# Four stacked graph-attention layers: score operands of layer 0 in PSUM, in place of one-instruction weights and woven block ends in layers 1 to 3

## The chip, the cores and the metric

The kernel runs on one core of a Trainium2 chip. The metric is device time in microseconds (us), from the first to the last instruction of one execution. Lower is better. A core has five engines that run side by side and wait for each other by semaphores: TensorE (PE, matrix products into PSUM; PEld is its loading of weights), VectorE (DVE, elementwise and reductions), ScalarE (ACT, one activation function with a scale and a bias), GpSimd (POOL; here it issues gathers and scatters by index) and SyncE (SP, issues plain transfers).

## The reference, cut to what matters

3327 nodes with 256 features; a symmetric 0/1 adjacency matrix with ones on the diagonal, with about 1% of its entries set. Each of four layers computes `x = layernorm(x + gnn(x, adj))`; the layers differ in how a pair's score is made.

```python
# layer 0: the score is not separable, a sum over 256 channels for each pair
g_src = x @ W_src.T + b_src;  g_tgt = x @ W_tgt.T + b_tgt
score = einsum('ijc,c->ij', leaky_relu(g_src[:, None] + g_tgt[None], 0.2), a_w)
gnn   = softmax(where(adj, score, -inf)) @ g_tgt

# layer 1: one head, e_ij = leaky_relu(s1_i + s2_j, 0.2)
Wh = x @ W.T;  s1 = Wh @ a1;  s2 = Wh @ a2
gnn = softmax(where(adj, e, NEG)) @ Wh

# layer 2: the same without the leaky_relu
# layer 3: two layers of 4 heads of 64 columns (called 3a and 3b here), each head as in layer 1
h   = einsum('nf,hfd->hnd', x, W)
e   = leaky_relu(f1[:, :, None] + f2[:, None, :], 0.2)
out = elu(einsum('hnm,hmd->hnd', softmax(where(adj, e, NEG)), h))   # 3b reads 3a's out
```

## The kernel before

Rows are handled in 26 tiles of 128 nodes.

**Layer 0** uses the sparse structure. For every tile it makes lists of neighbours (VectorE, from the adjacency matrix), sorts the rows of a group of tiles by the length of their lists, and gathers the neighbours' rows from DRAM by index. There are three groups, of 5, 8 and 13 tiles; `LEVELS` gives how many neighbours are gathered for each tile of a group after sorting (923 gathers of 128 rows in all). A tile's gathers are cut into parts of up to 8; there are 126 parts. `leaky_relu(s + t)` is written as `max(t, -s)` and terms that are linear.

```python
SETS = (5, 8, 13)
LEVELS = {5: (56, 38, 34, 32, 28), 8: (56, 40, ...), 13: (56, 41, ...)}
GROUP, TURNS, LEAD = 8, 11, 4

def gather(q):                       # GpSimd: one part
    if k0 == 0:
        own = io0.tile([P, OWN], F32, tag="own", name="own_of", bufs=4)
        nc.gpsimd.indirect_dma_start(out=own, in_=own_d[s], ...)
    g = gath.tile([P, GROUP, ROW], F32, tag=f"g{q % TURNS}", name="g")
    for k in range(k0, k1):
        nc.gpsimd.indirect_dma_start(out=g[:, k - k0, :], in_=table_d, ...)
        if k % 2 and between:
            between.pop(0)()         # a list written out, or a result put back

def largest(y, rows, minus_src, m):  # VectorE, four neighbours at once
    nc.vector.tensor_tensor(
        y, rows, minus_src[:, None, :].to_broadcast([P, m, dim]), op=ALU.max)

def weighted(y, sc):                 # VectorE, one neighbour: a score of each row
    nc.vector.scalar_tensor_tensor(
        y, y, 1.0, a_row, op0=ALU.mult, op1=ALU.mult, accum_out=sc)

# score(q): largest(..., own[:, :dim], m), then weighted(y, sc[...]) for each of the part
# combine(s, t): softmax weights, ScalarE scales each gathered row, TensorE adds them up
# add_input(s, t): divide, add the input; put_back(s, t): GpSimd scatters the rows
```

VectorE also makes the lists of the groups to come, spread over the parts that precede them. A group's lists are written out by GpSimd (`write_list`), once VectorE has ranked all its rows (`ranks_i`):

```python
for s in range(1, len(SETS)):
    at = begins[s] - LEAD - 1
    at_step(at, read_lists, s)
    at -= SETS[s] // 4 + 1
    for it in range(SETS[s]):
        at_step(at, between.append, lambda s=s, it=it: write_list(s, it))
    ahead.append(neighbours(s))
    owed[at] = steps                 # its lists are due by part `at`
```

**Layers 1 to 3** are dense. The output rows are cut into four blocks of 7, 7, 6 and 6 tiles. For a block, and for each of the 26 tiles `j` of source nodes (a step), a weight tile `e` is made and multiplied on TensorE. The exponential of a leaky_relu is split into factors of row and column, so that a weight is a maximum times the adjacency:

```python
def weigh(self, j, b, at, h_of):
    q = self.feat[j][:pn, ...]
    e = edges.tile([P, wide], F32, tag="e", name="e", bufs=8)
    nc.vector.scalar_tensor_tensor(
        e[:pn, : c1 - c0], self.rate[b][:pn, h_of, : c1 - c0], q,
        at[:pn, : c1 - c0], op0=ALU.max, op1=ALU.mult)
    return e
```

In layer 3, a block's end is short: ScalarE copies the accumulators out, and everything after is a generator in `pending`, advanced by one piece (`work_off`) in each step of the next block:

```python
def many_heads(layer, nxt, finish):
    for b, block in enumerate(blocks):
        work_until(lambda: layer.rate[b] is not None)
        accs = [[bank(3 * x + y) for y in range(pairs + 1)] for x in range(len(parts))]
        for j in range(nt):
            at = adjacent(j, b)
            es = [layer.weigh(j, b, at, h_of) for h_of in range(layer.nh)]
            # ... per part and head: products into accs[x][p] (L1184)
            # ... per part and head: sums of the weights into accs[x][pairs] (L1192)
            if j == 0 or j >= LATER:
                work_off()
        work_until(lambda: not pending)
        o = turn_p.tile([P, pairs, wide], F32, tag="ht", name="o")
        # ... nc.scalar.copy(o..., accs...), nc.scalar.copy(sums..., accs...)
        pending.append(finish(b, o, sums))
```

`finish_hidden` (3a) turns the sums so that rows lie on partitions (L1227), takes reciprocals of 28 or 24 columns (L1233), spreads them back by TensorE (L1266), multiplies, applies elu, and projects each tile for 3b (L998, then its rates, L1035), in stages of two tiles. `finish_last` (3b) turns the rows back (L1312), scales, applies elu, adds the residual, and normalises. The layer norms of layers 1 and 2 (`norms`) are such generators too, at the head of `prepare`, which turns (L1091) and projects (L998) each tile of a block for the next layer. In layer 3 the order of VectorE and ScalarE is the program's own; before it, that of TensorE alone is.

Of the kernel before, what the change touches and what calls it, by code (L numbers as in the profile page):

```python
# [32 lines left out]
SETS = (5, 8, 13)  # L33
LEVELS = {
    5: (56, 38, 34, 32, 28),
    8: (56, 40, 37, 35, 33, 31, 29, 27),
    13: (56, 41, 38, 37, 35, 34, 33, 32, 31, 30, 28, 27, 25),
# [9 lines left out]
def gat_stack(  # L47
# [84 lines left out]
    def dots(work, dst, weight, row, nh):  # L132

        for c in range(kc):
            t = work.tile([P, dim], F32, tag="spread", name="dots", bufs=4)
            nc.vector.tensor_mul(t, weight[:, c, :dim], row)
            nc.vector.tensor_reduce(
                dst[:, c, :], t.rearrange("p (h d) -> p h d", h=nh), axis=AX.X, op=ALU.add
            )
# [68 lines left out]
    def norms(block, ys):  # L208
# [4 lines left out]
        for s, it in enumerate(block):  # L213
# [4 lines left out]
            if s == len(block) // 2:  # L218
                yield
        yield from scaled(block, ys, mv)  # L220

    def scaled(block, ys, mv):
# [5 lines left out]
        yield  # L228
        for s, it in enumerate(block):
# [5 lines left out]
            if s == len(block) // 2:  # L235
                yield
        yield
# [12 lines left out]
    def sparse0(lost):  # L250
        GROUP, TURNS, LEAD = 8, 11, 4
        starts = [sum(SETS[:s]) for s in range(len(SETS))]
        with ExitStack() as s0:
# [3 lines left out]
            ps0 = s0.enter_context(tc.tile_pool(name="s_ps", bufs=2, space=PSUM))  # L257
            s0.enter_context(
# [89 lines left out]
            def sources(it):  # L348

                xt, pn = columns_of(it)  # L350
                pss = ps0.tile([P, BANK], F32, tag="ps", name="pss")
# [23 lines left out]
            def neighbours(s):  # L375
# [8 lines left out]
                for t in range(size):  # L384
# [7 lines left out]
                    for b, (lo, hi) in enumerate(halves):  # L392
# [23 lines left out]
                        for c in range(chunks):  # L416
                            if c == chunks // 2:
                                next(before if b else of_rows, None)
# [116 lines left out]

            def largest(y, rows, minus_src, m):
# [4 lines left out]
            def weighted(y, sc):  # L541

                nc.vector.scalar_tensor_tensor(  # L543
                    y, y, 1.0, a_row, op0=ALU.mult, op1=ALU.mult, accum_out=sc
# [9 lines left out]
            def score(q):  # L554
# [3 lines left out]
                own, g, kt = entry["own"], entry["g"][k0 // GROUP], places[s, t]  # L558
                y_own = None
                if k0 == 0:  # L560
# [9 lines left out]
                    largest(y_own, own[:, None, 2 * dim : 3 * dim], own[:, :dim], 1)  # L570
# [7 lines left out]
                for lo in range(k0, k1, 4):  # L578
# [3 lines left out]
                        y[:, :m, :], g[:, lo - k0 : lo - k0 + m, :dim], own[:, :dim], m  # L582
# [3 lines left out]
                if k0 == 0:  # L586
                    weighted(y_own[:, 0, :], sc[:, kt : kt + 1])
# [6 lines left out]
                for i, y in enumerate(ys):  # L594
                    weighted(y, sc[:, k0 + i : k0 + i + 1])
# [134 lines left out]

            for q, key in ends.items():
# [228 lines left out]
    def layers(rs):  # L960
# [15 lines left out]

        class Layer:
# [14 lines left out]
            def project(self, j, ht, banks):  # L992
# [10 lines left out]
                if self.leaky:  # L1003
                    f = feats.tile([P, dim + 2 * heads], F32, tag=f"{self.slot}{j}", name="feat")
                    nc.scalar.activation(f[:pn, dim : dim + nh], last, AF.Exp)
                    nc.scalar.activation(
                        f[:pn, dim + nh : dim + 2 * nh], last, AF.Exp, scale=SLOPE - 1.0
                    )
                    for lo in range(0, dim, width):
                        nc.scalar.activation(  # L1010
# [478 lines left out]
```

## Time and profile before

Three runs: 3377.6, 3378.3 and 3379.95 us; median 3378.3. The profiled execution spans 3378.2 us.

| engine | busy us | share |
|---|---|---|
| TensorE, products | 2265.2 | 67% |
| VectorE | 2332.9 | 69% |
| ScalarE | 722.5 | 21% |
| GpSimd | 1142.6 | 34% |

| stretch, us | stage |
|---|---|
| 0 to 180 | layer 0: table of target rows, lists of group 0 |
| 180 to 1618 | layer 0: gathers, scores, sums |
| 1618 to 1750 | layer 1 is prepared and begins |
| 1750 to 2304 | layers 1 and 2 |
| 2304 to 2841 | layer 3a |
| 2841 to 3378 | layer 3b, with a tail of 24 us after the last block |

The costliest groups (busy us; mean ns of one): gathers on GpSimd 1012.1 (1097); weights of layer 3 on VectorE 844.9 (1080); products of layer 3 on TensorE 663.5, its sums 333.5; weightings of layer 0 on VectorE 329.2 (419), maxima 278.5 (1180).

How to read it: the shares are averages over stages with different limits, so each part of the change has to be read in its own stretch. GpSimd works in layer 0 only; TensorE sets the pace only after it. The profile puts idle time down to what ended it: "issue" is idle time with nothing to wait for. A busy TensorE can hide a wait, as the ends of its products are modelled: a group of 16 that takes 4.68 us where others take 3.23 has waited inside.

### The profile page before, as it was taken

Reading aid. Unit: us, or ns where it says so; the run is one execution under the profiler, and the core shown is the slowest. Engines: PE = TensorE matmul, PEld = TensorE weight load, DVE = VectorE, ACT = ScalarE, POOL = GpSimd, SP = SyncE. Lnnn points to the kernel's source line nnn. Section 1 sums busy time; section 2 is a strip of 40 time slices with the busy share of each in tenths; the row PEclk is TensorE's granted clock in tenths of the full one; section 3 lists DMA queues with packets and bytes.
Section 4 is the critical chain, followed back from the end, with each engine's and each line's share of the span. In section 5 each row is a group of like instructions: output and inputs, shape, how many; then the busy total and the mean of one; then the engine's idle time right before and its main releaser. Section 6 shows DMA issues by size and latency. Waiting matters only on the chain.

```text
span 3378.2 us, 37935 instructions
## 1 busy us (share of the span) xinstructions
PE 2265.2 (67%) x12318; PEld 1185.5 (35%) x12318; DVE 2332.9 (69%) x6589; ACT 722.5 (21%) x1950; POOL 1142.6 (34%) x1034
## 2 busy tenths in 40 slices
PE   3203342533323443333799999999999999999997
PEld 2101111211111111111378888784333343333332
DVE  6789999999945555555235552117778788789997
ACT  0002221413212332333243431110110110110110
POOL 0177778777677777776000000000000000000000
PEclk6556675766666666766699999999999999999998
DMA  7465545444335333343367663332212212211111
GB/s 214 130 137 175 152 144 147 147 142 136 84 101 117 98 104 105 103 109 94 90 194 212 194 174 94 100 98 70 61 44 63 60 43 62 61 45 56 54 45 46
DMA packets 176816, 363.79 MB, mean 108 GB/s; under 512 B 33746, under 2 KB 118948, under 8 KB 176610
## 3 DMA queue, kind: packets, MB, share of 16 engines
q1 hardware_dynamic: 96682, 183.56, 19.2%
q0 software_dynamic: 49632, 141.57, 16.2%
q10 hardware_dynamic: 30296, 36.15, 3.1%
q8 instruction: 100, 1.64, 0.2%
q14 instruction: 106, 0.87, 0.1%
HBM read 320.99 MB, written 43.58 MB: 108 GB/s over the span
## 4 chain that ended last, share of the span: by engine, by line
PE 46%; DVE 4%; DMA 2%; ACT 1%; issue 1%; POOL 0%; DVEq 0%; ACTq 0%; POOLq 0%; SPq 0%
PE acc L1184 17%; PE acc L1146 14%; PE acc L1192 9%; PE misc L998 3%; DVE e L1062 2%; PE misc L1035 1%; DMA at_i<-in_adj_t_dram 1%; PE misc L1091 1%; DMA at<-at_d 1%; ACT feat L1010 0%; PE acc L626 0%; PE misc L1266 0%; PE misc L1227 0%; DVE stats L1341 0%; DVE h L1339 0%
## 5 line engine op out<-in xcount | busy, mean ns | idle before, releaser
L526 POOL DMA_INDIRECT g<-table_d,lst x923 | 1012.1, 1097 | 289.1 <-issue 269.7
L1062 DVE SCALAR_TENSOR_TENSOR e<-rate,feat,at 128x896 f32<-128x896 f32 (+4 forms) x832 | 844.9, 1080 | 100.9 <-PE acc L1192 91.8
L626 PE MATMUL acc<-g,ident 128*128 128x512 f32 (+1 forms) x936 | 455.1, 644 | 667.0 <-ACT g L623 611.1
L1184 PE MATMUL acc<-e,feat 128*64 128x384 f32 (+4 forms) x3328 | 663.5, 520 | 3.2 <-DVE e L1062 1.7
L225 POOL TENSOR_TENSOR rstds<-rstds,minus_half 128x7 f32<-128x7 f32 (+1 forms) x12 | 19.6, 1632 | 1711.0 <-DVE rstds L224 1711.0
L626 PEld LDWEIGHTS acc<-g,ident 128*128 128x128 f32 x936 | 194.2, 212 | 909.0 <-ACT g L623 671.8
L537 DVE TENSOR_TENSOR y<-g,own_of 128x1024 f32<-128x1024 f32 (+2 forms) x240 | 278.5, 1180 | 311.7 <-DMA g<-table_d,lst 293.2
L1184 PEld LDWEIGHTS acc<-e,feat 128*64 128x64 f32 (+1 forms) x3328 | 236.2, 136 | 391.7 <-issue 269.2
L623 ACT ACTIVATE g<-g,w 128x256 f32<-128x256 f32 x923 | 370.6, 493 | 0.0
L1192 PE MATMUL acc<-e,feat 128*32 128x384 f32 (+4 forms) x3328 | 333.5, 518 | 0.0
L543 DVE SCALAR_TENSOR_TENSOR y<-y,a_row 128x256 f32<-128x256 f32 x923 | 329.2, 419 | 0.0
L1146 PE MATMUL acc<-feat,e 128*128 128x257 f32 (+2 forms) x1352 | 308.3, 382 | 0.6 <-DVE h L1160 0.6
L1146 PEld LDWEIGHTS acc<-feat,e 128*128 128x128 f32 (+2 forms) x1352 | 253.8, 190 | 39.8 <-issue 4.1
L465 PE MATMUL key_rows<-key_diag,ones 128*128 128x128 f32 x52 | 18.3, 450 | 342.0 <-DVE key_diag L464 287.1
L1146 PE MATMUL acc<-feat,at 128*128 128x257 bf16 (+2 forms) x2028 | 241.1, 276 | 7.5 <-DMA at<-at_d 7.2
L612 ACT ACTIVATE w<-sc,top 128x57 f32<-128x57 f32 (+14 forms) x26 | 8.5, 326 | 1093.8 <-DVE top L609 1093.8
L1146 PEld LDWEIGHTS <-at 128*128 128x128 bf16 (+2 forms) x2028 | 200.3, 100 | 43.9 <-DMA at<-at_d 8.0
L1062 DVE SCALAR_TENSOR_TENSOR e<-rate,feat,at_i 128x896 f32<-128x896 f32 (+2 forms) x104 | 112.3, 1082 | 145.8 <-DMA at_i<-in_adj_t_dram 112.2
L420 DVE MAX8 cand<-num 128x8 f32<-128x64 uint16 x1352 | 179.5, 209 | 1.0
L1192 PEld LDWEIGHTS acc<-e,feat 128*32 128x32 f32 (+1 forms) x3328 | 86.6, 108 | 226.6 <-issue 226.6
L465 PEld LDWEIGHTS key_rows<-key_diag,ones 128*128 128x128 f32 x52 | 12.2, 284 | 356.9 <-DVE key_diag L464 266.9
L1079 ACT CAST at<-at_i 128x896 bf16<-128x896 int32 (+2 forms) x104 | 92.0, 885 | 112.6 <-DMA at_i<-in_adj_t_dram 111.0
(156 smaller groups left out, 1709.8 us busy)
## 6 DMA issues: line engine op xcount, KB each, us to landing
at<-at_d SPq DMA_DIRECT2D x150, 224.0 KB
at_i<-in_adj_t_dram SPq DMA_DIRECT2D x50, 448.0 KB
adj_i<-in_adj_dram SPq DMA_DIRECT2D x25, 832.0 KB
adj_i<-in_adj_dram SPq DMA_DIRECT2D x25, 831.5 KB
g<-table_d,lst POOLq DMA_INDIRECT x923, 2.9
at<-at_d SPq DMA_DIRECT2D x75, 192.0 KB
at<-at_d SPq DMA_DIRECT2D x75, 191.8 KB
at_d<-at ACTq DMA_DIRECT2D x50, 224.0 KB
```

Of the source, the lines that this page charges most:

```text
L420: nc.vector.max(cand[:, lo // CHUNK + c, :], v[:, c * CHUNK : (c + 1) * CHUNK])
L526: nc.gpsimd.indirect_dma_start(out=g[:, k - k0, :], out_offset=None, in_=table_d[:, :], in_offset=bass.IndirectOffsetOnAxis(ap=entry["lst" ...
L537: nc.vector.tensor_tensor(y, rows, minus_src[:, None, :].to_broadcast([P, m, dim]), op=ALU.max)
L543: nc.vector.scalar_tensor_tensor(y, y, 1.0, a_row, op0=ALU.mult, op1=ALU.mult, accum_out=sc)
L623: nc.scalar.activation(rows, rows, AF.Copy, scale=w[:, k : k + 1])
L626: nc.tensor.matmul(dst, ident, rows, start=start, stop=stop)
L998: nc.tensor.matmul(pacc[:pn, : dim + nh], ht[:, k, :pn], self.weight[:, k, :], start=(k == 0), stop=(k == kc - 1),)
L1062: nc.vector.scalar_tensor_tensor(e[:pn, : c1 - c0], self.rate[b][:pn, h_of, : c1 - c0], q, at[:pn, : c1 - c0], op0=ALU.max, op1=ALU.mult,)
L1079: nc.scalar.copy(at[:pn, :w], at_i[:pn, :w])
L1146: nc.tensor.matmul(accs[s][:pn, : dim + 1], a[:pj, s * P : s * P + pn], f[:pj, : dim + 1], start=(j == 0 and part == 0), stop=(j == nt - 1 ...
L1184: nc.tensor.matmul(accs[x][p][q * hd : (q + 1) * hd, : hi - lo], f[:pj, h_of * hd : (h_of + 1) * hd], es[h_of][:pj, lo:hi], start=(j == 0) ...
L1192: nc.tensor.matmul(accs[x][pairs][h_of * 32 : (h_of + 1) * 32, : hi - lo], f[:pj, dim + h_of : dim + h_of + 1].to_broadcast([pj, 32]), es[ ...
```

## The change

In **layer 0** the operands that all scores of a tile share, the negated source rows and the row `a_w`, are copied into a PSUM bank by ScalarE, so that the maxima and the weightings on VectorE read only one operand from SBUF. [...] The banks for it are taken from the sorting of the groups: a group may have 12 tiles at most, so the groups become 5, 9 and 12, and a tag of two banks keeps one.

```diff
-SETS = (5, 8, 13)
+SETS = (5, 9, 12)
...
-                pss = ps0.tile([P, BANK], F32, tag="ps", name="pss")
+                pss = ps0.tile([P, BANK], F32, tag="ps", name="pss", bufs=1)
...
+            def lay_out(q):
+                (s, t), _, _ = parts[q]
+                entry = held[s, t]
+                both = entry["both"] = ps0.tile([P, 2, dim], F32, tag="both", name="both")
+                nc.scalar.copy(both[:, 0, :], entry["own"][:, :dim])
+                nc.scalar.copy(both[:, 1, :], a_row)
...
-            def weighted(y, sc):
+            def weighted(y, sc, a):
...
+                minus_src, a = entry["both"][:, 0, :], entry["both"][:, 1, :]
...
+            for q, (key, k0, _) in enumerate(parts):
+                if k0 == 0:
+                    at_step(max(q - 2, 0), lay_out, q)
```

In **layers 1 and 3** a different scheme is taken out. The maximum is a relu on ScalarE and the product is VectorE's second half: `max(r q, 1) = relu(r q - 1) + 1`, with the factors of row and column exchanged to fit.

```diff
+                nc.scalar.activation(
+                    e[:pn, : c1 - c0], self.rate[b][:pn, h_of, : c1 - c0], AF.Relu,
+                    bias=minus_one[:pn], scale=q,
+                )
                 nc.vector.scalar_tensor_tensor(
-                    e[:pn, : c1 - c0], self.rate[b][:pn, h_of, : c1 - c0], q,
-                    at[:pn, : c1 - c0], op0=ALU.max, op1=ALU.mult,
+                    e[:pn, : c1 - c0], e[:pn, : c1 - c0], 1.0, at[:pn, : c1 - c0],
+                    op0=ALU.add, op1=ALU.mult,
                 )
```

A block's end in layer 3 is no longer woven into the next block. Reciprocals are taken of the accumulated sums as they lie (512 or 384 columns), and product and elu are made straight from the accumulators; the next block starts when nothing is pending. The norms are emitted at once, not in pieces, and VectorE and ScalarE are ordered by the scheduler in layer 3 too.

```diff
-                work_until(lambda: layer.rate[b] is not None)
+                work_until(lambda: layer.rate[b] is not None and not pending)
...
-                    if j == 0 or j >= LATER:
+                    if j >= LATER:
                         work_off()
                 work_until(lambda: not pending)
...
+                    inv = work.tile([P, BANK], F32, tag="invs", name="invs", bufs=1)
+                    nc.vector.reciprocal(inv[:, :w], accs[x][pairs][:, :w])
                     for p in range(pairs):
-                        nc.scalar.copy(o[:, p, lo:hi], accs[x][p][:, : hi - lo])
...
+                        spread = misc((6, 7))
+                        nc.tensor.matmul(
+                            spread[:, :w], select[:, p, :], inv[:, :w], start=True, stop=True
+                        )
+                        s = work.tile([P, BANK], F32, tag="spread", name="spread_s")
+                        nc.scalar.copy(s[:, :w], spread[:, :w])
+                        v = o[:, p, lo:hi]
+                        nc.vector.tensor_tensor(v, accs[x][p][:, :w], s[:, :w], op=ALU.mult)
+                        nc.vector.tensor_scalar_min(s[:, :w], v, 0.0)
+                        nc.scalar.activation(s[:, :w], s[:, :w], AF.Exp)
+                        nc.vector.scalar_tensor_tensor(
+                            v, s[:, :w], -1.0, v, op0=ALU.add, op1=ALU.max
+                        )
+                pending.append(finish(b, o))
...
-        def finish_hidden(b, o, sums):
+        def finish_hidden(b, o):
+            for it in blocks[b]:
+                l3b.project(it, o[:, :, at0 : at0 + P], (6, 7))
                 yield
             l3b.rates_of(b, o, (6, 7))
             yield
...
+        def finish_last(b, o):        # per tile: turn back on TensorE, add; then norms at once
...
-        rs.enter_context(
-            tc.manual_schedule(
-                engines={
-                    mybir.EngineType.PE, mybir.EngineType.DVE, mybir.EngineType.Activation
-                }
-            )
-        )
```

In a projection, the scaling of the features by their exponential is one VectorE instruction in place of one ScalarE instruction for each head (L1010). What is left out here is the text of the stages of `finish_hidden` and `finish_last` that go, and the loss of the `yield`s in `norms`.

## The prediction

> **What bounds the kernel now.** I read first the table of busy time by stretch, because one kernel holds four layers with different limits. Its columns: the stretch in us from the start, its length, busy us (and instructions) of PE, PEld, DVE, ACT and POOL, the granted TensorE clock, DMA share and GB/s.
>
> ```profile
> 300.00:500.00 200.00, 68.09 (x157) 32.89 (x155) 194.88 (x871) 44.27 (x113) 156.04 (x136) 0.65 0.52 152
> 900.00:1100.00 200.00, 72.07 (x153) 32.40 (x151) 107.98 (x401) 56.02 (x143) 155.20 (x149) 0.67 0.43 104
> ...
> 1750.00:1960.00 210.00, 209.41 (x979) 182.51 (x979) 116.99 (x234) 79.64 (x137) 4.27 (x3) 1.00 0.70 204
> 1960.00:2307.00 347.00, 336.30 (x2515) 281.35 (x2514) 78.95 (x224) 67.06 (x224) 5.59 (x4) 0.99 0.40 114
> 2307.00:2844.00 537.00, 534.78 (x3659) 194.41 (x3658) 439.22 (x462) 63.38 (x224) 2.10 (x1) 1.00 0.20 55
> 2844.00:3378.00 534.00, 514.24 (x3544) 183.56 (x3542) 468.71 (x569) 66.29 (x206) 7.63 (x4) 0.98 0.18 51
> ```
>
> Layer 0 (to 1620 us) has two parts. Until 889 us VectorE is 97% busy, as neighbour lists are made beside the scores; after that GpSimd alone is full: 155 us busy, and 0.30 us in front of each of its 149 instructions, which is 200 of 200. From 1750 us TensorE works without a gap.
>
> Next, the timeline of layer 0, GpSimd and VectorE: start, duration, engine, line, operation.
>
> ```profile
> 725.14 0.95 POOL L526 DMA_INDIRECT g<-table_d,lst  x1 [0.30 <-issue]
> 726.40 1.06 POOL L526 DMA_INDIRECT g<-table_d,lst  x1 [0.30 <-issue]
> 726.62 2.34 DVE L537 TENSOR_TENSOR y<-g,own_of 128x1024 f32<-128x1024 f32 x2
> 727.76 2.36 POOL L526 DMA_INDIRECT g<-table_d,lst  x1 [0.30 <-issue]
> ...
> 889.23 1.00 POOL L487 DMA_INDIRECT lists_d<-payload,ranks_i  x1 [9.79 <-DVE inv L648]
> ```
>
> A gather alone takes 0.95 us; the one beside two maxima with both inputs in SBUF takes 2.36. The last line is the hinge of the layer: GpSimd writes out the lists of group 2 only when VectorE has ranked them.
>
> Then a block's end in layer 3, TensorE only:
>
> ```profile
> 2444.98 1.71 PE L1192 MATMUL acc<-e,feat 127*32 127x512 f32 x16
> 2446.62 3.66 PE L1184 MATMUL acc<-e,feat 128*64 128x512 f32 x16
> 2450.21 1.71 PE L1192 MATMUL acc<-e,feat 128*32 128x512 f32 x16
> 2451.85 1.73 PE L1227 MATMUL misc<-heads_at,sums 128*128 128x4 f32 x14
> 2453.51 3.23 PE L1184 MATMUL acc<-e,feat 128*64 128x512 f32 x16
> ```
>
> A step is 3.23 + 1.71 less overlap, 4.80 us from start to start; between two blocks only 0.43 us is lost (3.66 for 3.23). The finish of a block lies piecemeal between the next block's steps.
>
> [...] `row<-pt,bt_row` from PSUM has median 418 ns, the `y_own` maximum from SBUF 416; `minus<-pss` from PSUM 406, the weighting from SBUF 420. [...] when layer 1 is prepared (1640 to 1660 us) the clock is 0.50, and a tile's projection takes 2.08 us where it takes 1.03 at 1.00:
>
> ```profile
> 1640.84 0.69 PE L1091 MATMUL misc<-ident,h 128*128 128x128 f32 x2 [0.77 <-ACT feat L1010]
> 1641.56 0.37 ACT L1094 COPY ht<-misc 128x256 f32<-128x256 f32 x1 [0.78 <-PE misc L1091]
> 1641.99 2.08 PE L998 MATMUL misc<-l1w,ht 128*128 128x257 f32 x4 [0.46 <-ACT ht L1094]
> ...
> 1644.84 0.69 PE L1091 MATMUL misc<-ident,h 128*128 128x128 f32 x2 [0.77 <-ACT feat L1010]
> ```
>
> One tile of such a chain, with one PSUM bank, takes 4.00 us. [...]
>
> ```profile
> L1233 DVE RECIPROCAL invs<-misc x8: 274/312/328, 2467.4 to 3355.7; 128x28 f32<-128x28 f32 x4, 128x24 f32<-128x24 f32 x2, 128x20 f32<-128x20 f32 x2
> ```
>
> 328 ns for 28 columns and 274 for 20 make about 7 ns a column.
>
> **The change in layer 0.** The maxima and the weightings read one operand from PSUM, so they stop holding up gathers. Three terms.
>
> (a) VectorE's full part. Groups of 9 and 12 tiles move the ranking of the last group from part 55 to part 59 (of 126). Four more parts cost 4 x 5.2 us (two maxima 2.28, eight weightings at 0.345, small ones 0.16) and one tile's combining 2.5: +23. Ranks: -1. The 4 us that VectorE waited for gathers go. So 889 becomes 907. [...]
>
> (b) GpSimd's full part. Before, 520 instructions from 889.2 to 1590.8: 1.349 us each. After, 448 gathers in place of 479, 487 instructions in all, at 0.95 + 0.30 and 10 us of waits: 619. So 917 + 619 = 1536 in place of 1591: **-55 us**.
>
> (c) ScalarE's two copies into PSUM a tile (26 x 2 x about 0.4) lie on an engine with 1094 us of idle time in this layer: 0.
>
> **The change in layers 1 to 3.** Weights take a second instruction, on ScalarE. From its 256-column form (0.403 us start to start) and 0.8 ns a column I estimate 0.92 us for 896 columns, 3.7 in a step of 4.80 (0.81, 3.25 in 4.16 for six tiles): it fits. VectorE still has one instruction of 1.07. What costs is the block end: a block now starts only when nothing is pending, normalising accumulators and ELU is done straight out of them, with reciprocals 512 and 384 wide.
>
> Seven-tile block of layer 3a, between its last matmul and the next block's first: VectorE, by the order of the built program, has two reciprocals (3.7 + 2.8), five weights (5.3), four products (2.4), four minima (1.3), four ELU ends (2.3), two feature scalings (1.0): 18.8. Then three projections at half clock (3 x 2.1) and two rate products (3.6 + 2.7, as in layer 1's preparation): 32; and 2.5 for the clock to come back: 34.5. The work that TensorE did before for the same finish between its steps, 15.0 (1.65 + 3.3 + 7.0 + 3.1), falls out: +19.5. Six tiles: 16.5 + 0.4 + 6.3 + 5.4 + 2.5 = 31 less 13.1, +18. Two of each: **+75**.
>
> Layer 3b: the same VectorE chain, then only transposes: 19 + 2 + 2.5 less 4.9 = 18.6, twice, and 21 less 4.2 = 16.8 once; 3 more as norms come ahead of weights: **+57**. Last block: 24 us of tail become 32: **+8**.
>
> Layer 2 to 3a: the last block of layer 2, of six tiles, must be normalised (9.5 us), turned and projected (6 x 4.00), and give its rates (7) before a step is made: 40.5 + 2, less 12.3 that was woven in: **+30**.
>
> What is gained back: from 2303.9 to 3354.2, 1050 us, there are 104 steps of 4.80 and 104 of 4.16 (931) and 82 of finishing work on TensorE; **37** were lost in steps that waited for weights because the finishes share VectorE (3.23 stretched to 4.68 or 5.16). These go. Layer 1: ScalarE has 0.94 + 0.92 + about 1.2 in a step of some 3.3 to 3.6: +5.
>
> Sum: 75 + 57 + 8 + 30 - 37 + 5 = +138; with layer 0, 138 - 55 = +83: 3378 + 83 = **3461 us**.
>
> **The rivals.** *Layer 0 wins.* If all 136 us of stretch (1012 less 923 x 0.95) came back, and TensorE kept its clock at the ends (about 50 less), the sum would be near -50: 3330. Against it: before 889 us VectorE is the limit, so stretch there is free. [...] *The weights' chain binds.* The eight buffers make ScalarE, then VectorE, refill within a step: by my count the fourth weight is there 5.5 us after its buffer is free and is needed after 6.0 (six tiles: 4.9 and 5.2). If it fails by 0.2 us a step, 208 steps add 40: 3500. *The ends are hidden after all.* If VectorE's chain overlaps better or the clock stays up, ends cost 10 each and the sum is near +20: 3400. TensorE's unbroken 534.78 of 537 leaves nothing for them to hide under, so I think it the less likely.
>
> **Range and chances.** The layer 0 term I trust to 25, the layer 3 terms to 35; together 40. So 3461, with 3405 to 3512 eight times in ten. 2% is 3446: slower by more 0.64, within 0.34, faster by more 0.02.
>
> **What would show it.** Right: gathers with mean near 0.95 to 0.98 (1.097 now); the last gather ends near 1536; the weighting still 420 ns; steps of 4.80 and 4.16 inside blocks; a hole of 28 to 35 us on TensorE at each of the ends of layer 3a, 20 to 24 in 3b, with clock 0.5; about 42 between layers 2 and 3. Wrong: [...] holes under 15, reciprocals of under 1 us, or steps over 5.

## The result, and the profile after

The changed kernel takes **3402.2 us** (median of 4 runs, 3399.8 to 3405.0) beside 3377.95 us for the kernel before: a ratio of **1.0072, 95% interval [1.0055, 1.009]**, 24 us slower. Predicted were 3461 us and a range from 3405 to 3512. The direction was right, the size (83 us) was 3.4 times too large.

First the table of busy time by stretch, of the changed kernel, with the columns explained in the prediction. Layer 0 now ends at 1540 us (1617 before) and layer 2 at 2242 (2304 before), so the stretches are cut at its own borders.

```profile
900.00:1100.00 200.00, 74.66 (x152) 33.36 (x152) 121.93 (x447) 63.24 (x162) 147.61 (x155) 0.66 0.46 108
...
2242.00:2282.00 40.00, 22.38 (x46) 9.77 (x48) 16.16 (x40) 4.44 (x20) 2.03 (x1) 0.56 0.07 18
2282.00:2836.00 554.00, 525.52 (x3469) 202.03 (x3466) 457.74 (x489) 437.97 (x494) 0.00 (x0) 0.97 0.19 53
2836.00:3372.00 536.00, 509.81 (x3416) 191.27 (x3419) 459.84 (x544) 422.59 (x448) 4.27 (x3) 0.96 0.18 49
```

In layer 0 GpSimd finishes 155 instructions in 200 us where it had finished 149. A stretch of 40 us between layers 2 and 3 is new, at a mean clock of 0.56. In layer 3 TensorE lost its unbroken row: 525.52 of 554.

The hinge of layer 0, from the timeline of the changed kernel (start, duration, engine, line, operation): a gather beside two maxima, and the first write of group 2's lists.

```profile
724.36 2.34 DVE L537 TENSOR_TENSOR y<-g,both 128x1024 f32<-128x1024 f32 x2
...
726.10 0.97 POOL L518 DMA_INDIRECT g<-table_d,lst  x1 [0.30 <-issue]
...
905.77 1.00 POOL L479 DMA_INDIRECT lists_d<-payload,ranks_i  x1 [10.34 <-DVE inv L649]
```

The gather that starts under the maxima takes 0.97 us where one took 2.36; the mean of all 923 is 0.989 us for 1.097. The lists come at 905.8 where they came at 889.2.

Last a block's end in layer 3a, TensorE alone, which answers to the block end of before:

```profile
2403.01 3.23 PE L1193 MATMUL acc<-e,feat 127*64 127x512 f32 x16
2406.17 1.71 PE L1201 MATMUL acc<-e,feat 127*32 127x512 f32 x16
2410.82 3.64 PE L1217 MATMUL misc<-invs,select 128*128 128x512 f32 x4 [2.94 <-DVE invs L1214]
2419.13 2.90 PE L1217 MATMUL misc<-invs,select 128*128 128x384 f32 x4 [4.67 <-DVE invs L1214]
2421.82 8.19 PE L1005 MATMUL misc<-l3bw,o 128*128 128x260 f32 x28
2429.94 3.17 PE L1043 MATMUL misc<-o,w_src 128*4 128x512 f32 x8
2433.04 3.23 PE L1193 MATMUL acc<-e,feat 128*64 128x512 f32 x16
```

From the end of the last step (2406.17 + 1.71 = 2407.88) to the next block's first product (2433.04) it is 25.2 us; 34.5 were predicted. TensorE waits for both reciprocals, the bracketed 2.94 and 4.67 us. The seven projections then take 8.19 us together, 1.17 each, where one takes 1.03 at full clock; and the products of the new block's first step take 3.23 us at once.

Added up by stage, from the first and last products of each stage in the two traces (spans 3378.2 and 3402.1):

| Stage | before | after | measured | predicted |
|---|---|---|---|---|
| layer 0, to its last accumulation | 1616.9 | 1539.8 | -77 | -55 |
| preparing layer 1 | 58.6 | 61.5 | +3 | 0 |
| layers 1 and 2 | 628.5 | 640.5 | +12 | +5 |
| gap ahead of layer 3 | 0 | 39.9 | +40 | +42.5 |
| layer 3 | 1050.3 | 1091.0 | +41 | +83 |
| tail | 23.9 | 29.4 | +5 | +8 |
| sum | | | +24 | +83 |

The predicted 83 in layer 3 is 75 + 57 for the ends, less 37 for the waits, less the 12.3 of work that leaves its first block, which the prediction had booked with the gap.

### The profile page after: what moved, and what is told of

The parts are those of the page before. It is cut to its first block, busy times and chain, and to the rows that moved or that the text cites. A ratio compares the mean times of both kernels' runs of the same rounds, so it can differ in the third digit from the quotient of the medians.

```text
span 3402.1 us, 38429 instructions
## 1 busy us (share of the span) xinstructions
PE 2284.6 (67%) x12068; PEld 1212.8 (36%) x12068; DVE 2372.5 (70%) x6714; ACT 1560.5 (46%) x2546; POOL 1027.9 (30%) x1034
## 3 DMA queue, kind: packets, MB, share of 16 engines
q1 hardware_dynamic: 96682, 183.56, 18.8%
## 5 line engine op out<-in xcount | busy, mean ns | idle before, releaser
L1068 ACT ACTIVATE e<-rate,minus_one,feat 128x896 f32<-128x896 f32 (+2 forms) x936 | 942.4, 1070 | 185.8 <-PE acc L1201 149.7
L518 POOL DMA_INDIRECT g<-table_d,lst x923 | 913.2, 989 | 297.4 <-issue 266.2
L1072 DVE SCALAR_TENSOR_TENSOR e<-e,at 128x896 f32<-128x896 f32 (+4 forms) x832 | 819.5, 1024 | 169.5 <-ACT e L1068 152.4
L1193 PE MATMUL acc<-e,feat 128*64 128x384 f32 (+4 forms) x3328 | 639.6, 525 | 0.0
L537 DVE TENSOR_TENSOR y<-g,both 128x1024 f32<-128x1024 f32 (+2 forms) x240 | 276.2, 1174 | 238.5 <-DMA g<-table_d,lst 222.6
L1193 PEld LDWEIGHTS acc<-e,feat 128*64 128x64 f32 (+1 forms) x3328 | 262.5, 138 | 366.5 <-issue 211.6
L543 DVE SCALAR_TENSOR_TENSOR y<-y,both 128x256 f32<-128x256 f32 x923 | 324.7, 417 | 0.0
L533 ACT COPY both<-own_of 128x256 f32<-128x256 f32 x26 | 9.7, 375 | 603.0 <-DMA own_of<-own_d,lst 469.8
L1072 DVE SCALAR_TENSOR_TENSOR e<-e,at_i 128x896 f32<-128x896 f32 (+2 forms) x104 | 105.8, 1022 | 136.3 <-DMA at_i<-in_adj_t_dram 76.8
L613 ACT ACTIVATE w<-sc,top 128x57 f32<-128x57 f32 (+15 forms) x26 | 8.5, 325 | 394.8 <-DVE top L610 339.4
```

Of the source, the lines that this page charges most:

```text
L518: nc.gpsimd.indirect_dma_start(out=g[:, k - k0, :], out_offset=None, in_=table_d[:, :], in_offset=bass.IndirectOffsetOnAxis(ap=entry["lst" ...
L537: nc.vector.tensor_tensor(y, rows, minus_src[:, None, :].to_broadcast([P, m, dim]), op=ALU.max)
L543: nc.vector.scalar_tensor_tensor(y, y, 1.0, a, op0=ALU.mult, op1=ALU.mult, accum_out=sc)
L1068: nc.scalar.activation(e[:pn, : c1 - c0], self.rate[b][:pn, h_of, : c1 - c0], AF.Relu, bias=minus_one[:pn], scale=q,)
L1072: nc.vector.scalar_tensor_tensor(e[:pn, : c1 - c0], e[:pn, : c1 - c0], 1.0, at[:pn, : c1 - c0], op0=ALU.add, op1=ALU.mult,)
L1193: nc.tensor.matmul(accs[x][p][q * hd : (q + 1) * hd, : hi - lo], f[:pj, h_of * hd : (h_of + 1) * hd], es[h_of][:pj, lo:hi], start=(j == 0) ...
```

## Experiments

The experiments ran on five chips. On four of them the kernel before took 3595 to 3658 us (medians) in place of 3375 to 3378. Traces of kernels with the same layers 1 to 3 agree there to 8 us on all chips; their layer 0 does not. (The kernel before has no trace on the four chips; that its difference too lies in layer 0 is inferred from this.) So what the runs say of layers 1 to 3 is read from stretches of their traces, or from runs on one chip; what they say of layer 0 is told apart by chip.

### Layers 1 to 3: the four combinations of weights and block ends

**Layer 0 of the change with the layers of before.**

```
 SETS, LEVELS, lay_out, largest, weighted, order of the fillers: as changed
 class Layer, one_head, many_heads, finish_*: as before
```

> Layer 0 of the changed kernel, layers 1 to 3 of the kernel before. My theory is that the two halves of the change add up: layer 0 ends 77 us earlier (last accumulation 1616.9 to 1539.8 in the two traces) and everything after it is as before, so 3378 - 77 = 3301 us (3294 to 3308). The rival, that part of the 77 is given back when layer 1 starts earlier, wants 3312 or more.

> As for the first run of it: layer 0 of the changed kernel, layers 1 to 3 of the kernel before. In undisturbed conditions 3378 - 77 = 3301 us (3294 to 3308); where the kernel before is itself at some 3595, it repeats 3703 within 15.

> Layer 0 of the changed kernel, layers 1 to 3 of the kernel before. Where the kernel before takes 3378: 3301 (3294 to 3308). Where it takes some 3610: 3680 to 3710, as twice already.

Measured: 3703.0, 3688.3 and 3723.7 us, beside 3595, 3617 and 3658 for the kernel before. All three fell on chips with the long layer 0, so whether it makes 3301 on the other kind stays open. From the last accumulation of layer 0 to the end the first run takes 1761.0 us (the others 1754.4 and 1755.5), and the kernel before 1761.3: what layer 0 gains or loses is not given back later.

**The weights alone, and the block ends alone.** Both on the changed layer 0; indices are left out here.

```
 # weights_alone: layers of before, woven ends, and in weigh():
-nc.vector.scalar_tensor_tensor(e, rate, q, at, op0=max, op1=mult)
+nc.scalar.activation(e, rate, AF.Relu, bias=minus_one, scale=q)
+nc.vector.scalar_tensor_tensor(e, e, 1.0, at, op0=add, op1=mult)
 # ends_alone: the changed kernel with these lines (and the two Exp scales) turned back
```

> Layer 0 of the changed kernel, layers as before except that a weight is ScalarE's relu and VectorE's product; block ends stay woven into the next block's steps. Against layer 0 alone (3301 expected): my theory gives ScalarE's weights only layer 1's +8 and up to +5 in layer 3, so 3305 to 3315. The rival, that the longer chain through ScalarE makes steps wait where the finishes use ScalarE too, wants +30 or more, 3330 and up.

> The changed kernel with a weight as one VectorE instruction again; layer 0 and the block ends stay as changed. My theory puts the loss of the layers (some +101) on the ends: about 8 us less than the changed kernel from layer 1 and 2 to 3 more for VectorE's slower form in the gaps, so 3392 to 3400. If the form of the weights makes the loss, it falls to 3320 or less.

Measured on one chip: layer 0 alone 3703.0, ends alone 3773.2, weights alone **4125.1**. From layer 0's last accumulation to the end: 1761.0 with neither, 1837.1 with the ends, 2188.4 with the weights; with both, on such chips, 1854.6 to 1859.0. So the ends cost 76 us, the two-instruction weights some 20 on top of them, and 427 where the ends stay woven, all of it in layer 3. The rival was right about the weights, by fourteen times its own figure. The timeline of weights_alone in the first block of layer 3 shows how:

```profile
2703.07 6.83 PE L1204 MATMUL acc<-e,feat 128*64 128x512 f32 x16 [3.37 <-DVE e L1082]
...
2711.47 0.44 PE L1111 MATMUL misc<-ident,h 128*128 128x128 f32 x2
2711.95 0.37 ACT L1114 COPY ht<-misc 128x256 f32<-128x256 f32 x1 [7.00 <-PE misc L1111]
2712.22 4.21 ACT L1078 ACTIVATE e<-rate,minus_one,feat 128x896 f32<-128x896 f32 x4
2713.38 4.17 DVE L1082 SCALAR_TENSOR_TENSOR e<-e,at 128x896 f32<-128x896 f32 x4 [7.31 <-ACT e L1078]
...
2714.53 6.24 PE L1204 MATMUL acc<-e,feat 128*64 128x512 f32 x16 [2.62 <-DVE e L1082]
```

ScalarE stands 7.00 us at one small copy of a transpose that TensorE only makes behind its whole step. In program order four relus lie behind that copy, VectorE waits 7.31 us for them and TensorE for VectorE: a circle, in which a step took some 11.5 us (2703.07 to 2714.53) in place of 4.80. Woven finishes and ScalarE's weights don't go together in this order of instructions. No run moved the copy alone, so what the change did to avoid the circle is told below (no_wait) only in part. That was not in my account at all: I had priced the weights by their busy time (four in 4.21 us, so they fit a step) and not by what stands in front of them.

The expectation for the ends alone was a miss as well: at most 10 us less than the changed kernel was expected, and it is some 20. Of these, 10 lie in layers 1 and 2 (625.9 for 635.5 to 636.2) and 6.5 in layer 3, whose six-tile blocks take 108.0 to 110.6 us in place of 109.4 to 111.9.

### Layer 3: what a block end consists of

These four edit the changed kernel. Each is read from the last product of layer 2 to the end: 1160.3 us in the first trace of the changed kernel, 1158.4 in the second, 1156.9 to 1160.3 in all nine traces with these layers. All but no_wait were timed once.

**Reciprocals narrowed, and made twice.**

```
-nc.vector.reciprocal(inv[:, :w], accs[x][pairs][:, :w])
+nc.vector.reciprocal(inv[:, :64], accs[x][pairs][:, :64])       # recip_64
+nc.scalar.activation(inv[:, 64:w], accs[x][pairs][:, 64:w], AF.Copy, scale=1e-9)
 # recip_twice: the reciprocal line stands twice
```

> The changed kernel with reciprocals of layer 3 narrowed to the first 64 of their 512 or 384 columns; ScalarE copies the rest, scaled by 1e-9, without inverting it (so the output is not the reference's). Read from the last product of layer 2 to the end, 1160 us in the changed kernel. My theory: VectorE's two reciprocals, 3.35 and 2.55 us, stand on the path of each of the eight block ends, so each loses 2.7 + 2.0: 38 less, 1122 (1115 to 1131). The rival, that TensorE's own 18 of the 25 us set the end, wants 1150 or more.

> The changed kernel with each reciprocal of layer 3 made twice. Same stretch, 1160 us in the changed kernel. My theory: + 3.35 + 2.55 at each of eight ends, 47 more, 1207; if the longer idle time of TensorE also leaves its clock at half during the projections of layer 3a, some 6 more at each of four ends, 1231. The rival wants 1175 or less.

Measured: 1122.4, 36 to 38 less, and 1212.1, 52 to 54 more. Both agree with the first theory: in sum, the two reciprocals stand on the path in full. (At a six-tile end both are 384 wide, so the sum of recip_twice is nearer 44 than 47. Single ends became 3.0 to 5.7 us shorter in recip_64, for 4.0 to 4.8 of narrower reciprocals.) The same end of a seven-tile block of 3a in recip_64, TensorE alone:

```profile
2803.14 1.71 PE L1201 MATMUL acc<-e,feat 127*32 127x512 f32 x16
2806.48 1.98 PE L1220 MATMUL misc<-invs,select 128*128 128x512 f32 x4 [1.63 <-ACT invs L1215]
2809.82 1.56 PE L1220 MATMUL misc<-invs,select 128*128 128x384 f32 x4 [1.36 <-ACT invs L1215]
```

The waits of 2.94 and 4.67 became 1.63 and 1.36, and with the shorter waits the four spread products take 1.98 us where they took 3.64. The doubled reciprocals lengthened the seven gaps by 6.2 to 8.2 us each, 0.3 to 2.3 more than their own time, and not by the further 6 in layer 3a that were expected of a half clock through all projections.

**TensorE kept busy while VectorE inverts.** The four products added write into a bank that nobody reads.

```
+keep = misc((6, 7))
+for _ in range(4):
+    nc.tensor.matmul(keep, ident, layer.rate[b][:, 0, :BANK], start=True, stop=True)
 for p in range(pairs):
```

> The changed kernel with four idle products (identity by a rate row, into a spare bank that nobody reads) ahead of each pair of spread products in a block end of layer 3, so that TensorE works while VectorE inverts. Same stretch, 1160 us in the changed kernel. If the half clock that the trace shows at the spread products (3.64 us for four) and at the first projections costs time, 3 to 4 less at each of seven ends: 1130 to 1140. If it costs nothing, as other engines set the pace there, 1155 to 1165.

Measured: 1150.6, 8 to 10 less, between the two. The same end, TensorE alone:

```profile
2797.55 1.88 PE L1222 MATMUL misc<-invs,select 128*128 128x512 f32 x4
2799.29 3.70 PE L1217 MATMUL misc<-rate,ident 128*128 128x512 f32 x8
2804.30 1.53 PE L1222 MATMUL misc<-invs,select 128*128 128x384 f32 x4 [1.31 <-DVE invs L1214]
2805.75 2.02 PE L1005 MATMUL misc<-l3bw,o 128*128 128x260 f32 x8
2808.15 1.15 PE L1005 MATMUL misc<-l3bw,o 128*128 128x260 f32 x4 [0.38 <-DVE feat L1016]
2810.00 3.92 PE L1005 MATMUL misc<-l3bw,o 128*128 128x260 f32 x16 [0.70 <-DVE feat L1016]
```

By the times of the spread products the clock stayed up: 1.88 us for 3.64, and 1.53 for 2.90. But the end shrank only from 25.2 to 22.9 us, because the projections now wait for VectorE's feature scalings (0.38 and 0.70), and the second spread still for its reciprocal. VectorE sets most of the pace here. The seven gaps together went from 146.8 to 138.5, 1.2 us an end. That is what this run got for the clock, not quite all that it is worth: the first spread also stood behind the added products, 0.7 us after its reciprocal was done (2796.9), and VectorE's instructions came in a slightly different order.

**No waiting for pending work.**

```
-work_until(lambda: layer.rate[b] is not None and not pending)
+work_until(lambda: layer.rate[b] is not None)
```

> The changed kernel, but a block of layer 3 starts as soon as its rates are there, although preparations are pending; they then lie between its steps. Read from the last product of layer 2 to the end, which takes 1160 us in the changed kernel. My theory: the 40 us gap ahead of layer 3 becomes some 5, and the 12 us of work in it reappear between the steps; at the other ends the projections only move; so 25 less in all, 1135 (1128 to 1142). The rival, that the work comes back in full as steps that wait for weights, wants 1155 or more.

Measured: 1136.7, as expected. The gap ahead of layer 3 is 0.3 us, and the gaps at the ends are 9 to 14 us in place of 17 to 25; what left them is found between the steps (the first block takes 146.3 us in place of 126.2, and layer 3 as a whole 1107.0 in place of 1091.0). So the wait costs 22 to 24 us: it removes 16 from layer 3 and adds 40 ahead of it. Here relus and a woven preparation do share ScalarE, without the circle of weights_alone. So the wait is not what avoids it. Other things differ, above all two: in the changed kernel's layer 3 the order of VectorE and ScalarE isn't fixed by the program, but chosen when it is built (TensorE's still is the program's), and a block's normalising is no longer among the woven pieces. Which of them it is, no run shows.

### Layer 0

**The changed kernel itself, once more, and with the two rows in SBUF.**

```
-both = entry["both"] = ps0.tile([P, 2, dim], F32, tag="both", name="both")
+both = entry["both"] = io0.tile([P, 2, dim], F32, tag="both", name="both")
```

> The changed kernel with one word altered: the tile with the two copied rows lies in SBUF instead of PSUM; groups, copies and order stay. If the place of the operand makes the gain, the gathers go back to a mean of 1.09 us and the 487 instructions from the last ranks on to 1.35 us each, 0.10 x 487 = +49, so 3445 to 3460. If the regrouping made it (groups of 5, 9 and 12), the time stays at 3400 to 3408 and the gathers stay near 0.99.

> The changed kernel unaltered, beside the kernel before, because in the first four runs the kernel before itself took 3595 us in place of 3378 and all of the difference lay in layer 0 (layers 1 to 3 took the same time to 1 us). If that call's chip or moment was disturbed and this one is not, before takes 3376 to 3380 and this 3400 to 3405. If the slow layer 0 belongs to the operands in PSUM on some chips, before is near 3595 and this kernel's layer 0 ends near 1935 us, which makes some 3797.

> As for the first run of it: the changed kernel with the two rows in SBUF. In undisturbed conditions 3445 to 3460 if the place of the operand makes the gain (gathers with mean 1.09 us, or a little more), 3400 to 3408 if the regrouping does.

Measured: both_sbuf 3586.4 (kernel before 3595); the changed kernel 3792.1 (kernel before 3617, ratio **1.0467 [1.0397, 1.0536]**), as expected for the case that the long layer 0 belongs to such a chip; both_sbuf_again, on the same chip, 3601.9 (ratio 0.9867 [0.9757, 0.9978]). On these chips the operands in PSUM make the kernel some 190 us longer (3792.1 for 3601.9), where I had expected 45 to 60 us of gain. The timeline of VectorE in the second run of the changed kernel shows what is different from the first:

```profile
206.19 0.23 DVE L412 MAX8 cand<-num 128x8 f32<-128x64 uint16 x1 [1.87 <-issue]
206.89 0.23 DVE L412 MAX8 cand<-num 128x8 f32<-128x64 uint16 x1 [0.47 <-issue]
207.59 0.23 DVE L412 MAX8 cand<-num 128x8 f32<-128x64 uint16 x1 [0.47 <-issue]
208.99 0.42 DVE L350 SCALAR_TENSOR_TENSOR minus<-pss,bs_row 128x256 f32<-128x256 f32 x1 [1.17 <-issue]
```

Instructions that depend on nothing new start 0.70 us or a multiple of it apart, and the bracket names no releaser ("issue"). From 160 to 400 us, 51 of 59 such waits end on one grid of 0.70 us; later ones lie on several. Counting VectorE's idle times of 0.3 to 2.5 us for which the profile names no releaser, from 160 us to the end of layer 0, gives some 340 of them, 369 us in all; in the first trace of the changed kernel there are 6, 10 us. VectorE's instructions themselves take no longer (a weighting 415 ns, 417 in the first trace).

**The groups alone, and each operand alone.**

```
 # groups_only: the kernel before with (LEVELS, one bank for pss and the order of the fillers to match)
-SETS = (5, 8, 13)
+SETS = (5, 9, 12)
 # max_psum:    minus_src, a = entry["both"][:, 0, :], a_row
 # weight_psum: minus_src, a = entry["own"][:, :dim], entry["both"][:, 1, :]
```

> The kernel before with groups of 5, 9 and 12 tiles and what the change needs for them (one bank for the source products, the two fillers swapped), no copies, operands in SBUF. Where the kernel before takes 3378, I expect 3365 to 3380, as GpSimd's part after the last ranks shrinks by 33 instructions of 1.35 and VectorE's part ahead of it grows by as much. Where the kernel before takes some 3610, as in both calls so far, its layer 0 should end with that of the changed kernel in SBUF, 1726 to 1751 us, so 3490 to 3515. If the copies and not the groups made that difference, it stays within 20 us of the kernel before.

> The changed kernel with the weightings' row read from SBUF again; the maxima keep theirs in PSUM (both copies are still made). Layer 0's last accumulation ends at 1540 us in the first trace of the changed kernel, at 1931 to 1944 in the later ones, at 1726 to 1751 with both rows in SBUF. Where the kernel before takes 3378: if the maxima alone stretched gathers (2.36 us for 0.95), this one keeps nearly all of the gain, 1540 to 1555. Where it takes some 3610: if the row of unbroken gathers holds VectorE up, it lies with the changed kernel, 1900 to 1945; if PSUM reads of the weightings do, near 1740.

> The converse: the maxima read their row from SBUF, the weightings theirs from PSUM. Where the kernel before takes 3378: gathers stretched as before, layer 0 ends at 1585 to 1610. Where it takes some 3610: with the maxima holding up gathers as in the kernel before, layer 0 ends at 1726 to 1770 if the row of gathers matters, at 1900 or more if PSUM reads do.

Measured: groups_only **3485.7**, beside 3630.7 for the kernel before: ratio 0.9669 [0.9557, 0.9781], with layer 0 ending where the expectation for such a chip has it. It is the one version that clearly beat both kernels on such a chip; on a chip like the first it was not run. max_psum took 3841.8 and weight_psum 3768.9, beside 3658.4 for the kernel before. Layer 0's end against the unexplained waits of VectorE, by run:

| Run | rows in PSUM | layer 0 ends | waits without a releaser |
|---|---|---|---|
| changed kernel, first trace | both | 1539.8 | 10 us |
| both_sbuf, both_sbuf_again | none | 1725.7, 1751.0 | 148, 189 |
| groups_only | none | 1735.2 | 169 |
| weight_psum | weightings' | 1906.8 | 274 |
| after_again | both | 1931.2 | 369 |
| l0_alone | both | 1944.4 | 344 |
| max_psum | maxima's | 1980.8 | 348 |

The 1751.0 comes from an execution 1.6% above the fastest of its kernel, so of the two values the first is the surer. The end goes with the waits. The maxima's operand does as much as both together, the weightings' alone somewhat less. By their expectations the two speak against each other: max_psum went the way of the unbroken row of gathers (1900 to 1945, and beyond), weight_psum the way of the reads from PSUM (1900 or more). The gathers' mean falls as the waits grow (1.10 us in groups_only, 1.05 in weight_psum, 1.00 in max_psum, 0.98 in after_again): the fewer gathers are stretched, the more VectorE stands. That is a going together, and no run shows it as the cause.

**GpSimd slowed down.** One memset of 64, 256 or 512 columns behind each gather.

```
 nc.gpsimd.indirect_dma_start(out=g[:, k - k0, :], ...)
+nc.gpsimd.memset(pace, 0.0)
```

> The changed kernel with one small memset on GpSimd (64 columns) behind each of the 923 gathers, which keeps the gathers apart. If the memset takes 0.2 to 0.3 us with its issue, the 487 instructions after the last ranks cost 100 to 150 more. Where the kernel before takes 3378, layer 0 ends at 1640 to 1690 in place of 1540. Where it takes some 3610: if the unbroken row of gathers holds VectorE up, layer 0 ends earlier than the 1931 of the changed kernel in spite of the added work, 1750 to 1880; if not, later, 1980 to 2090.

> As paced, with a memset of 256 columns behind each gather: a period of some 1.45 us in place of 1.25, as long as the mean with both rows in SBUF. Where the kernel before takes some 3610: if the unbroken row of gathers holds VectorE up, its waits without a cause in layer 0 fall from some 350 us to 200 or less and layer 0 ends at 1800 to 1900 in spite of 190 us of added GpSimd work; if not, the waits stay above 300 and it ends at 2000 or later.

> As paced_256, with 512 columns: a period of some 1.75 us, 1165 instructions of GpSimd in layer 0 then take 2000 us or so by themselves and set its end, 2050 to 2250. If the row of gathers holds VectorE up, its waits without a cause fall below 120 us; if not, they stay above 250.

Measured: paced 3802.6 beside 3658.4, with 346 us of waits and layer 0 ending at 1952. This says nothing of its question, since the memset of 0.17 us slipped into the 0.30 between two gathers and their period only went from 1.25 to 1.28 us. The other two were meant to settle it, but ran on a chip where the kernel before takes 3374.8 and VectorE has no such waits (5 and 4 of them, 8 and 9 us): 3528.8 and 3720.7 us. There they show something else: with periods of 1.44 and 1.65 us layer 0 ends at 1670.7 and 1859.7, 131 and 320 us later than with 1.25 (for paced_512, 2050 to 2250 and a period of 1.75 were expected: a miss). Of these, 42 and 137 lie ahead of the lists, which are written at 948 and 1042 us. Behind the lists, GpSimd's period is what layer 0 is made of on such a chip: to the last gather of paced_256, which starts at 1647.1, it is 699 us, or 1.44 for each of the 487.

## Why the prediction was too high

**The step that failed is the length of the block ends of layer 3.** Predicted were holes of 34.5 and 31 us in 3a, 23.5 and 21 in 3b, with clock 0.5 and 2.5 us for its return, 202 us over seven ends. Measured were 25.2, 24.1, 21.8 and 21.7, then 17.9, 19.2 and 16.9: 146.8. That is 55 us, and 13 came back, as the steps inside the blocks add up to 944 us where 931 were predicted. Two things in the 34.5 were wrong, by the end shown above (the other six, 4 to 10 us short each, are not taken apart here):

- *VectorE's chain was laid out in one row.* I put 18.8 us ahead of the projections: all reciprocals, weights, products, minima and ELU ends. The first projection starts 13.9 us after the last step (2421.82 - 2407.88). One of the five weights and the second half's products, minima and ELU ends ran beside projections, as the first projections need only the first half's columns. VectorE alone, of the changed kernel (L1072 is a weight, L1223 a product, L1227 an ELU end):

```profile
2420.04 2.09 DVE L1072 SCALAR_TENSOR_TENSOR e<-e,at 128x896 f32<-128x896 f32 x2
2422.04 0.56 DVE L1223 TENSOR_TENSOR o<-acc,spread_s 128x384 f32<-128x384 f32 x1
2422.51 1.09 DVE L1072 SCALAR_TENSOR_TENSOR e<-e,at 128x896 f32<-128x896 f32 x1
...
2425.99 0.56 DVE L1227 SCALAR_TENSOR_TENSOR o<-spread_s,o 128x384 f32<-128x384 f32 x1 [0.21 <-ACT spread_s L1226]
```

  The reciprocals themselves I had nearly right: 3.35 and 2.55 us where 3.7 and 2.8 were predicted, and the two runs on them show that all of it counts.
- *The clock was taken to be at half through the whole hole.* In the trace it is at half in part of it only. Three stretches of the same end:

```profile
2418.00:2421.00 3.00, 1.87 (x3) 1.17 (x4) 3.00 (x4) 0.21 (x1) 0.00 (x0) 0.50 0.00 0
2421.00:2424.50 3.50, 3.50 (x9) 2.39 (x8) 3.50 (x7) 1.39 (x5) 0.00 (x0) 0.51 0.00 0
2424.50:2428.00 3.50, 3.50 (x16) 2.47 (x15) 2.59 (x7) 1.24 (x7) 0.00 (x0) 1.00 0.25 66
```

  The third number from the end is the clock: 0.50, 0.51, then 1.00 from 2424.5 on, 5.4 us after TensorE went back to work at 2419.1 and in the midst of the projections. So projections and rates took 11.2 us for 12.6 (all seven projections, where I had counted three), and the next step began at a clock of 1.00 (2428 to 2433 us), without the 2.5 for its return. I had carried the half clock over from the preparation of layer 1, where each product waits for another engine. In these two traces the clock stayed at 0.50 through such a chain (1640 to 1660 us before, 2250 to 2282 after). It was at 1.00 again 4.6 to 5.4 us after a row of products without a break began: 1673.6 to 1678.7 before, 2279.9 to 2284.5 and 2419.1 to 2424.5 after. So the 2.5 is what such a return costs in the trace of before, 5.1 us at half clock; here that stretch had fallen on the spreads and projections already.

Together 18.8 - 13.9 = 4.9, 12.6 - 11.2 = 1.4 and 2.5 make 8.8 of the 9.3 us. The rest is in the sum itself: its terms, as they stand, make 33.9 and not 34.5.

This is the rival "the ends are hidden after all": this end of 3a costs 25.2 less the 15.0 of work that left the steps, 10 us, as that rival said, and all seven together 147 less 70, 11 each. That its total of 3400 nearly came true is in part luck: layer 0 gave 22 us more than predicted, while the steps of layer 3 cost 13 more and layers 1 and 2 cost 10 more. I gave it too little room because I looked at TensorE's full row for something to hide the ends under, while they hide under each other.

**Layer 0: right in kind, too small by 22 us.** The lists came at 905.8, which is the 907 of the working before I added 10 for PSUM reads; the weightings kept their time (417 ns; 419 with both inputs in SBUF). No trace had shown such a cost, and the trace of before spoke against it (418 ns for `row<-pt,bt_row` from PSUM, 416 for the `y_own` maximum from SBUF); the measurement decides, and it is 0 here. From there 487 instructions took 610 us, 1.25 each, without the 10 us of waits that I added. The two margins are the 20 us. In the same way of counting, the operands are worth (1.349 - 1.253) x 487 = 47 us and the groups the rest, some 28; this split is an estimate from the two traces, and no run on such a chip tested it. The paced runs support its factor, the period of a gather.

**The gap ahead of layer 3** was right (39.9 for 42.5), with its half clock (0.50 from 2250 to 2282 us): six tiles of 4.04 us each for 4.00. There each product does wait for another engine:

```profile
2252.53 2.10 PE L1005 MATMUL misc<-l3aw,ht 128*128 128x260 f32 x4 [0.52 <-ACT ht L1104]
2255.42 0.69 PE L1101 MATMUL misc<-ident,h 128*128 128x128 f32 x2 [0.79 <-DVE feat L1016]
2256.57 2.10 PE L1005 MATMUL misc<-l3aw,ht 128*128 128x260 f32 x4 [0.46 <-ACT ht L1104]
```

**Layers 1 and 2** cost 15 with their preparation for the 5 predicted. A relu was estimated at 0.92 us, with 0.8 ns a column, and four take 4.21, 1.05 each. (In the trace of before, ScalarE's copies in layer 3 take 372 ns for 256 columns and 586 for 512, 0.84 a column.) Turning the weights back gave some 20 us over all layers.

**The weights' chain** nearly holds its step: seven-tile blocks take 124.8 to 126.8 us, 26 steps of 4.80 making 124.8, with either form of weight; six-tile blocks are 0.5 to 1.4 us longer with the two-instruction form than in ends_alone. By the count of buffers that was expected. That the form of the weights and the unweaving belong together was not seen.

**The chances** leaned to slower by more than 2% (0.64) only because of the holes that were too long. On the other chips the change does cost more: 4.7%, 175 us, on that of after_again. Of these, 105 lie behind layer 0 (1859.0 less 1754.4 in l0_alone_again, which has the layers of before), and so the other 70 in layer 0, for a reason that no step of the prediction names.

## What to carry to other kernels

Price an instruction not only by its time but by what stands ahead of it on its engine: four relus that take 4.21 us of a step of 4.80 cost 427 us in all where small copies that wait for TensorE stand ahead of them. A gap on the engine that bounds need not be the sum of the chain that fills it; look which of the later pieces need only a part of the earlier ones, and don't carry a clock from a stage where every product waits (0.50 in the preparations here) to one where products come in a row (1.00 from 5.4 us into the row of this block end). And where a reciprocal stands on the path, make it narrow: the kernel before inverts 28 columns in 0.33 us, the changed one 512 in 3.35, and narrowing took 36 to 38 us off the kernel.

## What the runs showed of the hardware that was not expected

- A reciprocal on VectorE takes 2.55 us for 384 columns and 3.35 for 512: the difference makes 6.2 ns a column, where that of two weights (1.09 and 0.96 us for 896 and 768 columns) makes 1.0.
- One input in PSUM in place of SBUF cost VectorE nothing measurable: weightings 417 ns for 419 by the mean, maxima of 1024 columns 1215 ns for 1221.
- In layer 0 the same kernel took 1540 us on one chip and 1931 on another. On the latter VectorE had some 340 waits without a named releaser, the early ones of which end 0.70 us or a multiple of it apart, and over the runs on such chips the fewer gathers were held up, the more of it there was. What VectorE waits for there the trace doesn't show. Of the waits 84% have a gather in their time or up to 0.3 us before it, but so would 73% of stretches as long laid at random, so that tells little. Whether it is the unbroken row of gathers stays open, as the runs meant for it ran on a chip without the effect. A change in layer 0 of this kernel should be timed on both kinds of chip: the operands in PSUM gain on one (an estimate of 47 us, above), and lose some 200 us of layer 0 on the other.
